# A two-layer graph network on one core: expert results scattered to the tokens' places, and layer 1's edge loop in a written order

## The chip, the cores and the metric

The kernel runs on one core of a Trainium2 chip. The metric is the device time of the whole program in microseconds (us); lower is better. The core's engines are TensorE (PE; its weight loads are listed apart as PEld), VectorE (DVE), ScalarE (ACT), GpSimd (POOL) and SyncE (SP). Each runs its instructions in order. SP issues most of the transfers here, ACT some, and POOL issues all that are addressed by a list of indices.

## What is computed

There are 6250 nodes of 256 channels and 100000 edges, sorted by their destination. The network has two layers, and each has a graph part, an attention part and a mixture of experts (MoE).

```
xn = layernorm(x)
x  = x + gnn0(xn) + linear_attention(xn)         # layer 0
x  = x + moe0(layernorm(x))                      # 32 experts, the best one per token, relu
xn = layernorm(x)
x  = x + gat(xn) + mix(xn)                       # layer 1
x  = x + moe1(layernorm(x))                      # 16 experts, the best two per token
```
```
gat:  h = x @ W;  e = leaky(h_l[own] + h_r[other])         # 4 heads of 64
      att = softmax of e over the edges of one node;  out[own] += att * h[other]
mix:  k, v = layernorm of each of 8 heads of x;  out = x @ (k^T v / N) + x
moe1: y = x + sum of the 2 chosen experts' (relu(x w1 + b1) w2 + b2) * weight
      out = layernorm(y) * gamma + beta
```

In `moe1` the x inside is the layernormed token, so the experts' output is added to that token, normed once more, and then added to the stream.

## The kernel before

**Tiles.** The nodes make NT = 49 tiles of 128 rows (the last one is short). The stream `xs` lies in SBUF for most stages. The edges make TS = 782 tiles of 128. Layer 1's edge loop works in chunks of GT = 32 edge tiles (25 chunks), and each chunk in groups of 8 tiles (98 groups).

**Stages.** Load and first norm; layer 0's edge loop; dispatch of layer 0's experts ("f0"); these experts; the rows of layer 1 (`layer1_rows`); layer 1's edge loop; dispatch of layer 1's experts ("f1"); these experts; the final gather and layernorm.

**Dispatch and experts.** `dispatch` norms the tokens, computes the router's logits (PE, L352), takes the best one or two experts of each token, counts places within each expert, and scatters each normed token with an indirect DMA (L398, 128 rows a time) to its place in a list `f_xs`, which is ordered by experts. At its end (L462 to L467) it works out, for all tokens, in which row of the result list `f_ys` the token's result will stand (`pi`). The experts then take tile after tile of `f_xs`, with the weights of the tile's expert: two matmul layers on PE (L1797, L1809 for f1), a bias add on DVE, and a plain store of 128 results to `f_ys` in the experts' order (by ACT for f0, by SP for f1). Whoever needs the results fetches them with indirect gathers, 128 tokens a time, by `pi`: `layer1_rows` does so with 49 gathers, and the final stage with 98, two per tile of tokens. All gathers go through one helper at line 300, so its line stands for several tiles: `xg` (layer 0's edges), `h` (layer 1's edges) and `yg` (results).

**The final stage.** Per block of 7 token tiles it loads the normed tokens `xc`, which the dispatch stored; for each of 14 gathered tiles `yg`, DVE does `xc += yg * wt` (L1832). Then come the layernorm (L119 to L124), times gamma (L1836), plus beta (L1837), plus `xs` (L1838), and the stores.

**Layer 1's rows.** For each token tile: the result of f0 is added to `xs`, the norm is taken, its transposed form is stored to `xnT_d`, h = xn @ W is computed, and rows of h with its logits are stored to `h_d` by SP. `xs` itself goes to `xs1_d`.

**Layer 1's edge loop** has four parts per chunk.
- `fetch`: 32 indirect gathers on POOL into four buffers `h8` of 8 tiles each (7 such buffers in all); then the nodes' own logits of each edge: DVE makes one-hot rows `ST` (L1282) and weights `hw` (L1273, L1275), PE multiplies them (L1288), ACT copies the 4x512 results (L1290), and ACT's queue stores them to `al_d`.
- `own_part`: loads these logits in another layout.
- `weigh`: the running maximum over the edges of a node, made by scans on DVE (L1315 to L1376), then exp on ACT (L1379).
- `gain`, per group of 8 tiles: DVE multiplies the gathered rows by the weights into `w8` (L1404), makes the one-hot matrix `S` (L1410), PE sums the rows by node into a PSUM tile `ps` (L1415, 2 such tiles), and DVE adds the sum to two places of the accumulator `acc` (L1419).

A second stream of work, `keys_values`, is a generator. `beside.step()` at the end of each group advances it 1.36 steps on average. Its first half takes transposed tokens, centres each head with a matmul by a constant matrix `away` (L1174), and sums k^T v (L1199). Its second half multiplies the tokens by the resulting matrix `kvm` (L1233), adds this to `xs1` (L1236) and stores the sum to `xs2_d`, from where the stream is loaded after the loop.

**Order.** The framework's scheduler arranges the instructions within each engine from the program's order and the buffers' reuse, and inserts the semaphores. The program of the loop gathers one chunk ahead:

```python
held, most = fetch(*chunks[0]), None
...
for i, (t0, n) in enumerate(chunks):
    ahead = fetch(*chunks[i + 1]) if i + 1 < len(chunks) else None
    most = weigh(t0, n, alz, *held, most)
    if ahead:
        alz = own_part(*chunks[i + 1])
    gain(t0, n, held[0])
    held = ahead
beside.rest()
```

Of the kernel before, what the change touches and what calls it, by code (L numbers as in the profile page):

```python
# [52 lines left out]
def gps_kernel(ctx, tc, x, src, dst, edge_weight, g0_W, g0_b, m0_WqT, m0_WkvT, m0_WpT, m0_bp,  # L53
# [257 lines left out]
    def expert_slots(name, ne, nk):  # L311

        ns = (N * nk + ne * (P - 1)) // P
        rest = ns - N * nk // P
        xs_d = tc.dram_tile([ne * CAP + rest * P, C], F32, name=name + "_xs")
        ys_d = tc.dram_tile([ns * P, C], F32, name=name + "_ys")
        for d, j in [(xs_d, ne * CAP + j * P) for j in range(rest)] + \
                [(ys_d, j * P) for j in range(ns - rest, ns)]:
            nc.sync.dma_start(d[j:j + P, :], zero)
        return ns, xs_d, ys_d  # L320

    def dispatch(name, fb, fw, pps, ne, nk, bt, rw, rb, ns, xs_d, top, yi, finals, stored=None):

        mask = fb.tile([P, ne, bt + 1], F32, name="d_mask")
# [11 lines left out]
        kf = fb.tile([P, NT, nk], F32, name="d_kf")  # L338
        nc.vector.memset(kf[:, NT - 1, :], -1.0)

        def logits(t0):
            n = min(bt, NT - t0)
            finals(t0, n)
            xn = fw.tile([P, bt, C], F32, name="xn", bufs=3)
            layernorm(fw, xs[:, t0:t0 + n, :], xn, n)
            if stored is not None:
                nc.scalar.dma_start(stored[:, t0:t0 + n, :], xn[:, :n, :])
            lp = pps.tile([P, bt, ne], F32, name="lp")
            for i in range(n):
                xT = transposed(fw, pps, xn[:, i, :], "xT")  # L350
                for c in range(2):
                    nc.tensor.matmul(lp[:, i, :], xT[:, c, :], rw[:, c, :], start=c == 0, stop=c == 1)  # L352
# [5 lines left out]
        def put(t0, xn, lg, turn):  # L358
            n = min(bt, NT - t0)
            ti = fw.tile([P, bt, 8], U32, name="ti")  # L360
            full_ = n if t0 + n < NT else n - 1
            for i in range(n):
                r = rows(t0 + i)
                nc.vector.max(top[:r, t0 + i, :], lg[:r, i, :])
                nc.vector.max_index(ti[:r, i, :], top[:r, t0 + i, :], lg[:r, i, :])
            if full_:
                nc.vector.tensor_copy(kf[:, t0:t0 + full_, :], ti[:, :full_, :nk])
            if full_ < n:
                nc.vector.tensor_copy(kf[:LAST, NT - 1, :], ti[:LAST, full_, :nk])
# [3 lines left out]
                kf[:, t0:t0 + n, :, None].to_broadcast([P, n, nk, ne]), op=OP.is_equal)  # L373
# [20 lines left out]
            for i in range(n):  # L394
                t = t0 + i
                r = rows(t)
                for k in range(nk):
                    st = nc.gpsimd.indirect_dma_start(  # L398
                        out=xs_d, in_=xn[:r, i, :], in_offset=None,
# [45 lines left out]
        for e in range(0, ne, 8):  # L445
            q, eng = ((nc.sync, SP), (nc.scalar, ACT))[e // 8 % 2]
            for r in group_values(tail, e, eng, ne * CAP - P):
                st = q.dma_start(xs_d[ds(r, P), :], zero)
                tc.declare_no_dep(st.ins, group=name, reason="rows behind the tokens' ones")
                tc.add_to_no_dep_group(name, st.ins)  # L450

        sh = fb.tile([ne, ne], F32, name="d_sh")
        nc.vector.tensor_sub(gend, gend, gn[:, 0:1])
        nc.vector.tensor_scalar(gend, gend, float(P), None, op0=OP.mult)
        nc.vector.tensor_scalar(sh, ident[:ne, :ne], gend, None, op0=OP.mult)
        sp = pps.tile([P, ne], F32, name="lp")
        nc.tensor.matmul(sp, ones[:ne, :], sh, start=True, stop=True)
        ss = fb.tile([P, ne], F32, name="d_ss")
        nc.vector.scalar_tensor_tensor(ss, iota[:, :ne], -float(CAP), sp, op0=OP.mult, op1=OP.add)
        for k in range(nk):  # L460
            oh = fb.tile([P, NT, ne], F32, name="d_oh")
            nc.vector.tensor_tensor(oh, iota[:, None, :ne].to_broadcast([P, NT, ne]),  # L462
                                    kf[:, :, k:k + 1].to_broadcast([P, NT, ne]), op=OP.is_equal)
            nc.vector.tensor_tensor(oh, oh, ss[:, None, :].to_broadcast([P, NT, ne]), op=OP.mult)
            row_ = fb.tile([P, NT], F32, name="d_row")
# [1421 lines left out]
```

## Time and profile before

| what | us |
|---|---|
| time, 3 runs | 4258.5, 4259.78, 4265.85; median 4259.78 |
| the profiled execution | 4279.39 |
| its span, first to last instruction | 4277.6 |

The profiled execution is 19.6 us longer than the median. Its mean granted TensorE clock is 0.747. The stages in it:

| stage | from | to | us |
|---|---|---|---|
| load and norm | 0 | 136 | 136 |
| layer 0's edge loop | 136 | 1325 | 1189 |
| f0 dispatch | 1325 | 1484 | 159 |
| f0 experts | 1484 | 1701 | 217 |
| layer 1's rows | 1701 | 1878 | 177 |
| layer 1's edge loop | 1878 | 3425 | 1547 |
| f1 dispatch | 3425 | 3621 | 196 |
| f1 experts | 3621 | 4101 | 480 |
| final gather and layernorm | 4101 | 4278 | 177 |

The profile's lines are read like this. A group (part 5 of the page) names line, engine, operation, tiles (output <- inputs) and count; after the bar stand the busy time, the mean time of one instruction in ns, the idle time of the engine just before instructions of that group, and what ended most of that idle time. The releaser "remote" means that a semaphore from elsewhere ended it, and "issue" that nothing the profile shows did. A timeline has start, length, engine and line, and in brackets the idle time before with its releaser. A line of the stretches has, for each engine, busy us and the number of instructions, then the granted clock, the share of DMA time and GB/s.

### The profile page before, as it was taken

The numbers are of one execution on the slowest core, as the hardware profiler recorded it, in microseconds if no ns is written. First come the engines' busy times: TensorE is split into PE (matmuls) and PEld (weight loads), VectorE is DVE, ScalarE is ACT, GpSimd is POOL, SyncE is SP. The second block draws the span as 40 slices with busy tenths as digits, with TensorE's granted clock in tenths as the row PEclk, the third lists the DMA queues.
The fourth block names the chain that finished last, engine by engine and source line by source line (L and its number), as shares of the span: only waits on it lengthen the run. The fifth ranks groups of instructions, "written<-read, shape, count | busy, mean of one in ns | idle before, by whom it ended". The sixth has DMA issues, their size and how long they took to land. (4 is left out here: it accounts for less than half of the span.)

```text
span 4277.6 us, 40881 instructions
## 1 busy us (share of the span) xinstructions
PE 2514.4 (59%) x10553; PEld 1822.0 (43%) x10553; DVE 2102.2 (49%) x6180; ACT 596.0 (14%) x1582; POOL 1826.0 (43%) x1864
## 2 busy tenths in 40 slices
PE   5455655677776487654554554555454444999920
PEld 4334444555555354531323333332233333888820
DVE  5345444445445666833544554554454654222247
ACT  3100000000001122221221221011010011222200
POOL 0566666566562400434445444544554245000046
PEclk9777877777786565777777777677786655999965
DMA  6643333233331344764433443454453163655644
GB/s 201 193 124 104 105 102 101 83 97 96 100 96 38 133 141 118 200 169 126 124 114 110 128 117 103 123 160 140 131 144 84 44 251 134 185 182 182 185 149 128
DMA packets 371451, 560.63 MB, mean 131 GB/s; under 512 B 106308, under 2 KB 259557, under 8 KB 370943
## 3 DMA queue, kind: packets, MB, share of 16 engines
q0 software_dynamic: 89760, 245.19, 20.5%
q1 hardware_dynamic: 243446, 273.73, 20.4%
q10 hardware_dynamic: 37992, 38.89, 2.8%
q8 instruction: 93, 1.52, 0.2%
q14 instruction: 160, 1.30, 0.1%
HBM read 440.48 MB, written 117.09 MB: 130 GB/s over the span
## 5 line engine op out<-in xcount | busy, mean ns | idle before, releaser
L300 POOL DMA_INDIRECT h<-h_d,idx x782 | 745.1, 953 | 814.2 <-DVE brk L1266 238.9
L300 POOL DMA_INDIRECT xg<-xw_d,idx x782 | 756.4, 967 | 550.0 <-issue 211.9
L1415 PE MATMUL ps<-w,S 128*128 128x260 f32 x1564 | 432.1, 438 | 374.4 <-DVE S L1410 256.7
L1415 PEld LDWEIGHTS ps<-w,S 128*128 128x128 f32 x1564 | 335.3, 219 | 488.5 <-DVE S L1410 281.8
L300 POOL DMA_INDIRECT yg<-f_ys,pi x147 | 168.3, 1145 | 813.1 <-SPq L1820 490.9
L802 PE MATMUL ps<-xg,S 128*128 128x256 f32 x1564 | 457.4, 439 | 81.2 <-DVE S L799 45.7
L802 PEld LDWEIGHTS ps<-xg,S 128*128 128x128 f32 x1564 | 333.4, 225 | 166.3 <-issue 59.1
L805 DVE SCALAR_TENSOR_TENSOR acc<-ps,in,acc 128x256 f32 x392 | 187.7, 479 | 387.6 <-remote 234.0
L1419 DVE SCALAR_TENSOR_TENSOR acc<-ps,in,acc 128x260 f32 x196 | 94.3, 481 | 556.6 <-remote 525.1
L1288 PE MATMUL p<-ST,hw 128*4 128x512 f32 x392 | 230.2, 700 | 178.9 <-DVE ST L1282 71.1
L398 POOL DMA_INDIRECT f_xs<-xn,d_pi x147 | 155.6, 1059 | 250.5 <-ACT xT L133 78.0
L799 DVE TENSOR_SCALAR S<-iota,lo,wt 128x128 f32<-128x128 f32 x782 | 242.9, 349 | 0.1
L1404 DVE TENSOR_TENSOR w<-h,exi 128x2048 f32<-128x2048 f32 x98 | 222.7, 2272 | 11.7 <-ACT exi L1379 11.7
L1809 PE MATMUL y<-w,h 128*128 x856 | 215.0, 392 | 11.2 <-ACT h L1802 10.1
L1797 PEld LDWEIGHTS hT<-xTt,w 128*128 128x128 f32 x1712 | 211.4, 194 | 6.1 <-ACT xTt L133 0.5
L1797 PE MATMUL hT<-xTt,w 128*128 128x128 f32 x1712 | 212.1, 277 | 0.2 <-ACT xTt L133 0.2
L1290 ACT COPY a<-p 4x512 f32<-4x512 f32 x196 | 111.3, 571 | 662.2 <-PE p L1288 272.3
L1805 DVE TENSOR_SCALAR h<-hT,b1T 128x128 f32<-128x128 f32 x214 | 74.8, 350 | 253.2 <-ACT h L1802 252.4
L1809 PEld LDWEIGHTS y<-w,h 128*128 128x128 f32 x856 | 149.0, 189 | 45.6 <-ACT h L1802 23.5
L1288 PEld LDWEIGHTS p<-ST,hw 128*4 128x4 f32 x392 | 24.1, 88 | 315.2 <-issue 147.7
L749 PE MATMUL ctx<-v,k 128*128 128x129 f32 (+1 forms) x196 | 44.2, 362 | 172.4 <-ACT v L747 118.2
L131 PE MATMUL tr<-ident,xt 128*128 128x128 f32 x350 | 84.7, 330 | 89.0 <-DMA xt<-f_xs 88.2
(344 smaller groups left out, 3979.3 us busy)
## 6 DMA issues: line engine op xcount, KB each, us to landing
w<-in_L_ffn_w SPq DMA_DIRECT2D x123, 512.0 KB
lob<-lob_d SPq DMA_DIRECT2D x97, 512.0 KB
xT<-xnT SPq DMA_DIRECT2D x196, 128.0 KB
xt<-f_xs SPq DMA_DIRECT2D x107, 128.0 KB
f_ys<-y SPq DMA_DIRECT2D x107, 128.0 KB
xnT<-xT SPq DMA_DIRECT2D x98, 128.0 KB
xg<-xw_d,idx POOLq DMA_INDIRECT x782
h<-h_d,idx POOLq DMA_INDIRECT x782
```

The source lines that it names most:

```text
L300: nc.gpsimd.indirect_dma_start(out=o, out_offset=None, in_=tab, in_offset=bass.IndirectOffsetOnAxis(ap=idx, axis=0))
L398: st = nc.gpsimd.indirect_dma_start(out=xs_d, in_=xn[:r, i, :], in_offset=None, out_offset=bass.IndirectOffsetOnAxis(ap=pi[:r, t, k:k + 1] ...
L799: nc.vector.tensor_scalar(S[:, i, :], iota, lo0[:, t:t + 1], wt0[:, t:t + 1], op0=OP.is_equal, op1=OP.mult)
L802: nc.tensor.matmul(ps, S[:, i, :], xg[:, i, :], start=i == 0, stop=i == n - 1)
L805: nc.vector.scalar_tensor_tensor(a, ps, m[:, b:b + 1], a, op0=OP.mult, op1=OP.add)
L1288: nc.tensor.matmul(p4[:, :w], hw, ST[:, j:j + w], start=True, stop=True)
L1290: nc.scalar.copy(a4[:, :w], p4[:, :w])
L1404: nc.vector.tensor_tensor(w8[:, :m, :C].rearrange("p i (k d) -> p i k d", k=4), hg[u // 8][:, :m, :C].rearrange("p i (k d) -> p i k d", k= ...
L1415: nc.tensor.matmul(ps, S[:, i, :], w8[:, i, :], start=i == 0, stop=i == m - 1)
L1419: nc.vector.scalar_tensor_tensor(a, ps, k[:, q:q + 1], a, op0=OP.mult, op1=OP.add)
L1797: nc.tensor.matmul(hT[:, f, :], w1[:, c, f * P:(f + 1) * P], xT[:, c, :], start=c == 0, stop=c == 1)
L1809: nc.tensor.matmul(yp, h[:, f, :], w2e[:, f * C:(f + 1) * C], start=f == 0, stop=f == nf - 1)
```

## The change

It has two parts.

**Results scattered by the experts' tiles.** Each row of `f_xs` gets extra words behind its 256 channels: the row in `f_ys` where this token's result belongs and, for f1, the token's weight for this expert and a flag that is 1 in its first copy and 0 in its second. Rows without a token carry a row number beyond the list. The dispatch so makes one normed tile per choice, copied on ACT, and works out the weights per group of tiles instead of once at its end; the search for result rows (L462 to L467) goes. A tile of experts scatters its results with an indirect DMA on POOL (`give_back`) to the tokens' places. For f1 it multiplies by the weight first and adds the token times its flag, so the normed tokens are no longer stored. `layer1_rows` and the final stage load results with plain transfers on SP (`results`), 4 and 7 tiles at once. In the final stage one add per block replaces 14 multiply-adds. The beta term is added to `xs` beside the experts.

**Layer 1's loop.** Its order is now the written one (`manual_schedule`), with gathers two chunks ahead. The product is made in place in `h8` (8 buffers), so there is no `w8`. `ps` and `S` have four buffers, and the sums of a chunk are added to `acc` during the next one (`added`). Own logits of a chunk go to one PSUM tile of 32 rows, with one copy and one store. In `keys_values` the heads are centred on DVE from rows `xr_d`, which `layer1_rows` stores by ACT's queue; its second half moves into the dispatch of f1 (`finals`), its rate is 1.1, and the stream is loaded from `xs1_d`.

The diff, cut to its core:

```diff
+    def give_back(name, ys_d, xt, y):
+        st = nc.gpsimd.indirect_dma_start(
+            out=ys_d, in_=y, in_offset=None,
+            out_offset=bass.IndirectOffsetOnAxis(ap=xt.bitcast(I32)[:, C:C + 1], axis=0),
+            bounds_check=ys_d.shape[0] - 1, oob_is_err=False)
...
+    def results(t, ys_d, k, t0, n):
...
+            nc.sync.dma_start(t[:, :whole, :], ys_d[r0:r0 + whole * P, :].rearrange(
+                "(t p) c -> p t c", p=P))
...
             finals(t0, n)
-            xn = fw.tile([P, bt, C], F32, name="xn", bufs=3)
-            layernorm(fw, xs[:, t0:t0 + n, :], xn, n)
-            if stored is not None:
-                nc.scalar.dma_start(stored[:, t0:t0 + n, :], xn[:, :n, :])
+            xn = [fw.tile([P, bt, rw_], F32, name=f"xn{k}", bufs=2 if nk == 2 else 3) for k in range(nk)]
+            layernorm(fw, xs[:, t0:t0 + n, :], xn[0][:, :, :C], n)
+            for k in range(nk):
+                if k:
+                    nc.scalar.copy(xn[k][:, :n, :C], xn[0][:, :n, :C])
+                nc.vector.tensor_copy(xn[k].bitcast(I32)[:, :n, C], ids[:, k, t0:t0 + n])
...
+            if nk == 2:
...
+                nc.scalar.activation(df[:, :n], df[:, :n], AF.Exp)
...
+                nc.vector.tensor_mul(xn[1][:, :n, C + 1], df[:, :n], xn[0][:, :n, C + 1])
...
-        for k in range(nk):
-            oh = fb.tile([P, NT, ne], F32, name="d_oh")
...
-            nc.vector.tensor_tensor(yi[:, k * NT:(k + 1) * NT], row_, pi[:, :, k], op=OP.add)
...
-                        nc.scalar.dma_start(ys_d[i * P:(i + 1) * P, :], y)
+                        give_back(name, ys_d, xt, y)
...
-                for t in range(t0, t0 + n):
-                    yg = mw.tile([P, C], F32, name="yg", bufs=8)
-                    gather(yg, ys_d, pi[:, t:t + 1])
-                    nc.vector.scalar_tensor_tensor(xs[:, t, :], yg, 0.0, xs[:, t, :],
-                                                   op0=OP.max, op1=OP.add)
+                yg = mw.tile([P, 4, C], F32, name="yg")
+                results(yg, ys_d, 0, t0, n)
+                nc.vector.scalar_tensor_tensor(xs[:, t0:t0 + n, :], yg[:, :n, :], 0.0,
+                                               xs[:, t0:t0 + n, :], op0=OP.max, op1=OP.add)
...
+                nc.scalar.dma_start(xr_d[:, t0:t0 + n, :], xn[:, :n, :])
...
-                                    nc.tensor.matmul(cen[:, t, h, :], xT[:, t, h, :], away,
-                                                     start=True, stop=True)
+                            nc.vector.tensor_reduce(sm[:, :8 * n], heads(xr), AX.X, OP.add)
+                            nc.vector.scalar_tensor_tensor(heads(xr), over(sm), -1.0 / 32, heads(xr),
+                                                           op0=OP.mult, op1=OP.add)
...
-                    h8 = gw.tile([P, 8, CR], F32, name="h8", bufs=7)
+                    h8 = gw.tile([P, 8, CR], F32, name="h8", bufs=8)
...
-                        p4 = pps.tile([4, 4 * P], F32, name="p4", bufs=2)
-                        nc.tensor.matmul(p4[:, :w], hw, ST[:, j:j + w], start=True, stop=True)
-                        a4 = gw.tile([4, 4 * P], F32, name="a4")
-                        nc.scalar.copy(a4[:, :w], p4[:, :w])
...
+                        nc.tensor.matmul(p4[:, :w], hw[:, i, :], ST[:, j * P:j * P + w],
+                                         start=i == 0, stop=i == nj - 1)
+                a4 = gw.tile([32, 4 * P], F32, name="a4")
+                nc.scalar.copy(a4, p4)
...
+            def added(t0, pss):
...
-                    w8 = gw.tile([P, 8, CR], F32, name="w8", bufs=2)
...
+                    next(due, None)
...
-                    ps = pps.tile([P, CR], F32, name="ps", bufs=2)
+                    ps = pps.tile([P, CR], F32, name="ps", bufs=4)
...
-            beside = Steps(keys_values(), 1.36)
+            beside = Steps(keys_values(), 1.1)
...
+            with tc.manual_schedule():
+                hgs, lgs, most, due = [], [], None, iter(())
+                for i in range(len(chunks) + 2):
+                    if i >= 2:
+                        t0, n = chunks[i - 2]
+                        most, fc = weigh(t0, n, hgs[i - 2], own_part(t0, n), *lgs[i - 2], most)
+                        due = gain(t0, n, hgs[i - 2], fc, due)
+                    if i < len(chunks):
+                        hgs.append(rows_to(*chunks[i]))
+                        lgs.append(own_logits(*chunks[i]))
+                for _ in due:
+                    pass
+                beside.rest()
...
-        nc.sync.dma_start(xs[:, t0:t0 + CH, :], xs2_d[:, t0:t0 + CH, :])
+        nc.sync.dma_start(xs[:, t0:t0 + CH, :], xs1_d[:, t0:t0 + CH, :])
...
+                            nc.vector.tensor_add(xs[:, t:t + m, :], xs[:, t:t + m, :], mix[:, :m, :])
...
+                            nc.vector.scalar_tensor_tensor(y, y, xt[:, C + 1:C + 2], xf,
+                                                           op0=OP.mult, op1=OP.add)
+                            give_back("f1", ys_d, xt, y)
...
-                            gather(yg, ys_d, pi[:, k * NT + t:k * NT + t + 1])
-                            nc.vector.scalar_tensor_tensor(xc[:, t - t0, :], yg, wt[:, k, t:t + 1],
-                                                           xc[:, t - t0, :], op0=OP.mult, op1=OP.add)
+                    xc, yg = (fw.tile([P, CH, C], F32, name=q, bufs=3) for q in ("xc", "yg"))
+                    for k, q in enumerate((xc, yg)):
+                        results(q, ys_d, k, t0, CH)
+                    nc.vector.tensor_add(xc, xc, yg)
```

## The prediction

> **What bounds the kernel now.** I read the stretches first (busy time of each engine per stage), because the change touches three stages that have different limits. Columns: stretch, its length, busy us (instructions) of PE, PEld, DVE, ACT, POOL, granted TensorE clock, DMA share, GB/s.
>
> ```profile
> 1980.00:3425.00 1445.00, 730.76 (x2448) 448.68 (x2447) 746.70 (x1927) 196.24 (x469) 691.24 (x726) 0.75 0.41 117
> 3425.00:3621.00 196.00, 82.22 (x364) 72.39 (x364) 109.73 (x521) 24.59 (x65) 102.91 (x98) 0.50 0.55 196
> 3621.00:4101.00 480.00, 430.92 (x2782) 380.67 (x2782) 119.72 (x321) 105.17 (x321) 0.00 (x0) 0.98 0.57 176
> 4101.00:4278.00 177.00, 0.00 (x0) 0.00 (x0) 119.80 (x273) 3.38 (x8) 117.27 (x98) 0.51 0.48 148
> ```
>
> These are layer 1's edge loop (it begins at 1878, where the gathers of its first chunk go out; 1547 us in all), the dispatch of its experts, the experts, and the final gather with the layernorm. In the loop no engine is busy much over half the time, so something waits in turn. The experts are PE's (431 of 480). The end is DVE and POOL in alternation.
>
> Then the groups, to see what the loop's POOL and DVE wait for; the last column is idle time before the group and its releaser.
>
> ```profile
> L300 POOL DMA_INDIRECT h<-h_d,idx x782 | 745.1, 953 | 814.2 <-DVE brk L1266 238.9
> L1404 DVE TENSOR_TENSOR w<-h,exi 128x2048 f32<-128x2048 f32 x98 | 222.7, 2272 | 11.7 <-ACT exi L1379 11.7
> L1419 DVE SCALAR_TENSOR_TENSOR acc<-ps,in,acc 128x260 f32 x196 | 94.3, 481 | 556.6 <-remote 525.1
> ```
>
> POOL's 782 gathers stand idle for 814 us. DVE stands idle for 557 us before its adds of the group sums. Last the timelines of POOL, PE and DVE around one chunk's end:
>
> ```profile
> 2531.38 0.94 POOL L300 DMA_INDIRECT h<-h_d,idx  x1 [0.30 <-issue]
> 2555.35 1.17 POOL L300 DMA_INDIRECT h<-h_d,idx  x1 [23.03 <-DVE w L1404]
> ```
> ```profile
> 2520.45 3.56 PE L1415 MATMUL ps<-w,S 128*128 128x260 f32 x15 [2.39 <-issue]
> 2524.34 0.38 PE L1415 MATMUL ps<-w,S 128*128 128x260 f32 x1 [0.34 <-issue]
> ```
> ```profile
> 2537.70 0.49 DVE L1419 SCALAR_TENSOR_TENSOR acc<-ps,in,acc 128x260 f32 x1 [17.12 <-remote]
> ```
>
> A gather run of POOL ends at 2532.3, then POOL idles 23 us until DVE's product L1404 frees a buffer of rows. DVE had stood at L1419 for 17 us although PE's records of these sums end at 2524.7. It went on 5.4 us after the gather run ended. The same distance stands at three other chunk ends (runs ending at 2153.2, 2219.2, 2283.3; adds at 2158.6, 2224.5, 2288.7). So a sum reaches DVE late while POOL issues gathers back to back, and DVE, stopped there, does not free POOL's buffers. Each chunk is 40 us of gathers and some 22 us of POOL waiting, 62 us in all; why the sums are late the trace does not show.
>
> **The loop after.** Removed: `added` takes a chunk's sums during the next chunk (four ps buffers), so the stop at L1419 goes. The product is made in the gathered rows, so a row buffer is freed by PE's last matmul of its group rather than by DVE, and eight buffers hold two chunks. What is late next:
> - POOL: gathers back to back take 0.95 + 0.30 = 1.25 us (the timeline), 32 of them 40 us. 782 x 1.25 = 978 us is the floor.
> - DVE per chunk, from the rows by form: four groups of product 2.28, S 1.22, two adds 0.96, ST 0.75, hw 0.43: 5.6 x 4 = 22.6, less some 2 where instructions overlap; weigh about 10.5 (2538.1 to 2548.5 in the timeline, with others' work between); keys_values at 1.1 steps a group, 4.4 a chunk, one tile pair: sum 0.68, centring 0.68 (priced by the 128x512 add), sum of squares 0.68, two u at 0.415, small ones 0.4: 3.3. Together 33 to 36, below 40.
> - PE: the rows L1415 (432.1 busy) and L1288 (230.2) make 662 in the loop, 27 a chunk, and both stay; PE is not the bound. ACT's copies of logits fall from 8 of 0.57 to 1, SP gains nothing but xr rows in place of xT.
>
> The new wait: POOL's gather of chunk i waits for PE's matmuls of chunk i-2. Queued behind it are only later gathers. DVE can start weigh 5 us after a run has ended (landing), the product of group 0 some 14 later, so PE has freed the first buffer near 26 to 30 of the next run's 40 us. If that release comes at once, POOL never stops: 978 plus ends. If it comes as late as DVE's sums did, POOL stops at the run's end and goes on 5 us later. The rows nearest are exactly those 5.4, 5.4, 5.3 and 5.5 us, so I take one pause of 5 per chunk: 45 x 24.4 chunks = 1100. To this come the start and the tail: last rows landing 5, the rest of gain, weigh and gain again 23 + 24, adds 2: about 55. **Loop 1155, so -392.** From below: no pause, some 1035 to 1060. From above: DVE's fixed order idles at every ACT exp and at each late release twice a chunk, 50 to 52 us a chunk, 1270 to 1330.
>
> **The end.** Ninety-eight gathers go (98 x 1.25 = 122 us of POOL), seven loads of two 0.9 MB tiles come in on SP. DVE loses L1832 (98 x 0.477, 45.1) and the bet adds (14.1, now beside the experts), gains seven adds at 2.0 (14.1): 119.8 - 45.1 = 75. Traffic is 12.8 MB in and 6.4 out, at 200 to 250 GB/s (the best slices of the page) 77 to 96. Start and last store 10 to 20. I take **100, so -77** (-85 to -60).
>
> **Dispatch of layer 1's experts** (196). Added: the mixing matmuls, 196 at 0.33 = 65 us of PE, which is 82 of 196 busy, so mostly beside; 25 adds at 0.68 = 17 of DVE; thirteen copies of the second row on ACT; per group of four an Exp beside the layernorm's Sqrt, two table loads of 1.28 (that row) = 33 of ACT, where DVE waits for both; some 10 of small DVE work. Removed: the closing L462-L467 (six of 0.97 and two small: 6) and 6.4 MB of xn stores. Scatters stay 98. POOL has 98 x 1.35 = 132 there. I take **+30**; below +10 if ACT and PE hide, +60 if nothing does.
>
> **The rest.** Experts f1: a multiply-add on DVE (0.48) and a copy on ACT (0.37) per tile of 4.5 us, a scatter of about 1 us on a POOL that does nothing there (0.00), in place of SP's store: 0, from -5 to +15 (the xt rows grow by 3 words, and the result leaves one step later). Experts f0: the store leaves ACT's queue for POOL's: 0 +- 5. Layer 1's rows (177): 49 gathers, 13 stores on ACT's queue and 13 loads of 512 KB on SP's; DVE's work there stays: -5, from -15 to +15. The zero stores at the start, 48 fewer: 0 to -10, taken as 0. Sum: -392 - 77 + 30 - 5 = -444. The profiled execution took 4279.4, so 3835; it is 19.6 above the median of the runs, 4259.8, so on that footing **3815**.
>
> **Rivals.**
> 1. *DVE's fixed order is the bound* (50 to 52 a chunk, loop 1300). For it: 36 us of work against 40 leaves 4 for all its waits on ACT, and nothing may be reordered. Against: DVE's waits besides L1419 are short (11.7 before L1404 in total). Time 3815 + 150 = 3965.
> 2. *The sums still stop the loop* (it does not do what it says). If the late release grows with the time since the last pause, PE's buffers come free no sooner than DVE's did: the loop stays near 1500, time 4165. For: the worst lag in the waits is 25.7 us. Against: POOL then has a pause, and a pause is what released the sums.
> 3. *Slower: POOL and the compute in lockstep.* Rows' landings may be seen as late as the sums. Then weigh of chunk i-2 begins only when the run of i-1 is over, both sets of buffers are full, and POOL waits for landing 5 and most of DVE's 33: 40 + 5 + 33 = 78 a chunk, 1903 in the loop, +356 - 52 = about 4565. It decides as soon as no group has been freed when a run ends, and costs over 62 a chunk once 22 us of compute are left then. For: z L1315 also waits for h rows, 56 us in 14 waits. Against: the longest of these is 6.7.
> 4. *DVE against POOL at SBUF.* In the end, beside the two-input ops L1836 to L1838, gathers took 2.0 instead of 0.95:
> ```profile
> 4140.74 2.03 POOL L300 DMA_INDIRECT yg<-f_ys,pi  x1 [0.30 <-issue]
> ```
> In a loop bounded by POOL each two-input DVE op that is new there would stretch a gather by its length: 25 x (0.68 + 0.83) = 38, time 3853. Against: inside the loop the mean gather is 0.953 even with L1404 and two-input adds around it. The Trainium skill, "SBUF — State Buffer", section "Who interferes with whom", says that a VectorE instruction with two SBUF inputs contends with a GpSimd instruction that reads SBUF. This trace agrees at 4140 and hardly inside the loop.
>
> **Chances.** Forecast 0.56 (its own range 3690 to 3900: loop 1060 to 1210 with the other terms' bounds), DVE's order 0.17, SBUF 0.07, late sums 0.10 (a fifth of it, 0.02, within 0.2% because the dispatch costs its bound too and the loop gains nothing), lockstep 0.08, below 3690 0.02. Range 3690 to 4080: it takes in rivals 1 and 4 and leaves out about 0.2. Faster by over 0.2% (about 8.5 us, what a measurement of this kernel can tell from no change): 0.90; within 0.02; slower 0.08.
>
> **What would show it.** Right: POOL's idle before the row gathers falls from 814 to about 250 and its releaser is PE's matmul; DVE's "remote" before the delayed adds is gone; the loop is 1155 long; the mean gather stays 0.95; the end has no indirect gathers and lasts 100; the dispatch is longer by 30. Wrong: DVE over 90% busy in the loop (rival 1), POOL pauses of 20 us per chunk (2) or of 35 with DVE's z waiting for rows (3), gathers of 1.2 us and more (4). The prediction falls first with the assumption that a late release costs a pause of 5 us and not more.

## The result, and the profile after

The changed kernel took 4159.65 us (median of 4 runs, 4132.14 to 4211.6), the kernel before 4260.17 beside it. The ratio is 0.974, with an interval of 0.9685 to 0.9795. A ratio with an interval leaves out, here and below, runs that are over 1.5% longer than the same kernel's fastest. The forecast was 3815 with a range of 3690 to 4080, so a gain came, of 100 where 445 was forecast. The profiled execution is the longest of the four: 4211.6, with a span of 4209.8. Its stages against those of the profiled execution before (us):

| stage | before | after | difference | forecast |
|---|---|---|---|---|
| load, norm, layer 0's loop, f0 dispatch | 1484 | 1500 | +16 | 0 |
| f0 experts | 217 | 232 | +15 | 0 |
| layer 1's rows | 177 | 208 | +31 | -5 |
| layer 1's loop | 1547 | 1350 | -197 | -392 |
| f1 dispatch | 196 | 270 | +74 | +30 |
| f1 experts | 480 | 548 | +68 | 0 |
| end | 177 | 102 | -75 | -77 |
| sum | 4278 | 4210 | -68 | -444 |

The stretches after, in the columns used before (stretch, length, busy us of PE, PEld, DVE, ACT, POOL, clock, DMA share, GB/s):

```profile
1940.00:3290.00 1350.00, 642.83 (x2156) 411.23 (x2156) 855.08 (x2074) 139.10 (x342) 781.95 (x783) 0.74 0.43 123
3290.00:3560.00 270.00, 121.19 (x558) 107.49 (x558) 124.06 (x633) 63.59 (x110) 102.47 (x98) 0.55 0.44 144
3560.00:4108.00 548.00, 437.85 (x2782) 382.84 (x2782) 183.99 (x435) 156.59 (x428) 104.66 (x107) 0.97 0.51 153
4108.00:4210.00 102.00, 0.00 (x0) 0.00 (x0) 78.32 (x177) 3.39 (x8) 0.82 (x1) 0.51 0.56 189
```

The experts' PE does the same 430 to 438 us of work as before, and stands still for the rest of a stage that is 68 longer. In the loop DVE is busy for 63%, POOL for 58%: again something waits in turn. The groups that answer to the three shown of before, first POOL's from the page, then DVE's from the groups of this stretch:

```profile
L300 POOL DMA_INDIRECT h<-h_d,idx x782 | 781.7, 1000 | 713.9 <-issue 399.0
```
```profile
L1435 DVE TENSOR_TENSOR h<-h,exi 128x2048 f32<-128x2048 f32 x98 | 222.9, 2274 | 3.4 <-ACT exi L1394 2.1 <-issue 1.3
L1422 DVE SCALAR_TENSOR_TENSOR acc<-ps,in,acc 128x260 f32 x196 | 95.2, 486 | 5.0 <-DVE acc L1422 0.9 <-PE ps L1445 0.7
```

DVE's idle time before the adds fell from 557 to 5, as forecast. POOL's fell only from 814 to 714, where 250 was said; but 210 of the 714 is one wait ahead of the loop's first gather, since POOL has no work left in layer 1's rows (64 before). Inside the loop its pauses of over 1 us fell from 521 to 274. The waits inside the loop (engine, line, what it waited for, us in total, times, longest):

```profile
ACT a L1306 <- remote: 507.3, 15, 39.3
DVE fc L1401 <- ACT fc L1399: 204.5, 17, 23.5
```

In place of DVE at the adds, ACT now waits in front of L1306, its copy of the own logits, and DVE waits for ACT. One chunk shows how. First PE, then ACT, DVE and POOL:

```profile
2576.48 7.05 PE L1303 MATMUL p<-ST,hw 128*32 128x512 f32 x16 [0.47 <-issue]
2616.64 9.59 PE L1445 MATMUL ps<-h,S 128*128 128x260 f32 x29 [33.10 <-DVE S L1440]
```
```profile
2608.51 0.57 ACT L1306 COPY a<-p 32x512 f32<-32x512 f32 x1 [36.38 <-remote]
2609.45 1.28 ACT L1394 ACT_TABLE_LOAD   x1 [0.37 <-ACT a L1306]
2610.75 1.00 ACT L1394 ACTIVATE exi<-z 128x32 f32<-128x32 f32 x4
```
```profile
2592.65 0.31 DVE L1391 STREAM_TRANSPOSE z<-zl 128x128 f32<-128x128 f32 x1
2611.91 0.23 DVE L1401 TENSOR_SCALAR fc<-fc,in 128x4 f32<-128x4 f32 x1 [18.95 <-ACT fc L1399]
```
```profile
2604.03 0.95 POOL L300 DMA_INDIRECT h<-h_d,idx  x1 [0.30 <-issue]
2624.12 0.95 POOL L300 DMA_INDIRECT h<-h_d,idx  x1 [19.14 <-issue]
```

PE's records of the logits end at 2583.5. POOL's run (gathers without a pause between them) ends at 2605.0. ACT's copy starts at 2608.5, 25 us behind PE and 3.5 behind POOL. The exps of the next chunk stand behind that copy in ACT's queue, though their inputs were ready at 2593.0 (L1391). DVE needs the exps, so its products come 19 us late, PE frees POOL's buffer late, 0.7 us before the next gather, and POOL pauses 19 us. This chunk takes 61 us. In the last third of the same loop the runs fell otherwise. ACT's copy mostly starts as soon as PE is done, here at 2812.8, 17 us into a run of POOL, and the pause is the one forecast:

```profile
2812.88 0.58 ACT L1306 COPY a<-p 32x512 f32<-32x512 f32 x1 [12.68 <-PE p L1303]
```
```profile
3065.30 0.95 POOL L300 DMA_INDIRECT h<-h_d,idx  x1 [0.30 <-issue]
...
3072.05 0.94 POOL L300 DMA_INDIRECT h<-h_d,idx  x1 [4.55 <-issue]
```

Most chunks up to 2744 take 59 to 61, those after 2840 mostly 45 to 48. How many take which differs from one execution to the next, and with it the time.

### The profile page after: what moved, and what is told of

It reads as the page before. It is cut to its first block, busy times and chain, and to the rows that moved or that the text cites. A ratio compares the mean times of both kernels' runs of the same rounds, so it can differ in the third digit from the quotient of the medians.

```text
span 4209.8 us, 40726 instructions
## 1 busy us (share of the span) xinstructions
PE 2422.2 (58%) x10353; PEld 1803.2 (43%) x10353; DVE 2218.2 (53%) x6303; ACT 617.3 (15%) x1577; POOL 1877.2 (45%) x1894
## 5 line engine op out<-in xcount | busy, mean ns | idle before, releaser
L300 POOL DMA_INDIRECT h<-h_d,idx x782 | 781.7, 1000 | 713.9 <-issue 399.0
L1445 PE MATMUL ps<-h,S 128*128 128x260 f32 x1564 | 445.1, 445 | 674.6 <-DVE S L1440 455.7
L1445 PEld LDWEIGHTS ps<-h,S 128*128 128x128 f32 x1564 | 344.1, 225 | 782.4 <-DVE S L1440 474.4
L326 POOL DMA_INDIRECT f_ys<-y,xt x175 | 180.1, 1029 | 633.0 <-DVE y L1855 418.3
L1435 DVE TENSOR_TENSOR h<-h,exi 128x2048 f32<-128x2048 f32 x98 | 222.9, 2274 | 3.4 <-ACT exi L1394 2.1
L1303 PE MATMUL p<-ST,hw 128*32 128x512 f32 x392 | 178.4, 604 | 34.7 <-DVE ST L1298 17.8
L139 PE MATMUL pr<-wp,aT 128*128 128x256 f32 x196 | 73.5, 512 | 125.1 <-ACT aT L133 63.9
L131 PEld LDWEIGHTS tr<-ident,xt 128*128 128x128 f32 x350 | 44.4, 160 | 222.6 <-issue 206.8
```

The source lines that it names most:

```text
L131: nc.tensor.transpose(p[:, c, :], t[:, c * P:(c + 1) * P], ident)
L300: nc.gpsimd.indirect_dma_start(out=o, out_offset=None, in_=tab, in_offset=bass.IndirectOffsetOnAxis(ap=idx, axis=0))
L326: st = nc.gpsimd.indirect_dma_start(out=ys_d, in_=y, in_offset=None, out_offset=bass.IndirectOffsetOnAxis(ap=xt.bitcast(I32)[:, C:C + 1], ...
L1303: nc.tensor.matmul(p4[:, :w], hw[:, i, :], ST[:, j * P:j * P + w], start=i == 0, stop=i == nj - 1)
L1435: nc.vector.tensor_tensor(v, v, ex[:, u:u + m, :, None].to_broadcast([P, m, 4, 64]), op=OP.mult)
L1445: nc.tensor.matmul(ps, S[:, i, :], h8[:, i, :], start=i == 0, stop=i == m - 1)
```

## The experiments

The theory: PE's results are seen late while POOL issues gathers back to back (shown for part of each run, see the last section); the change removed DVE's stop behind them and put ACT's copy, with the exps behind it, in the same place. The rival: DVE's fixed order sets the chunk. For the other stages: buffers that scatters hold too long, against wider rows or more work.

The runs went to two kinds of chip. On one the kernel before takes 4260 to 4270, as in the first runs; on the other 3851 to 3854. All ten traces of the first kind have waits put down to "remote" (138 to 202 in each), and none of the eight of the other has one. A time is compared only with the kernel before on its own chip, and "4260" and "3850" name the kinds below.

**results_only** (on 3850): the results part, with the loop of before.

> Only the results part of the change; layer 1's loop, the mix add and the stream's store are those of before. Theory A (the profile of after read by stages): final stage about 102 instead of 177 (-75), experts f1 548 instead of 480 (+68), f0 experts and layer 1's rows +15 and +31, dispatch f1 +10 to +30, so some 4310 +- 30, slower than before. Theory B (the losses in the experts' stages come with the loop part, which leaves other data and other buffers behind): final stage -75 alone, some 4185.

3962.68 against 3854.48, ratio 1.0268 (1.0234 to 1.0303). The part is a loss of 108 by itself: the end takes 102, the f1 experts 551. Theory A.

**loop_only** (on 3850): the loop part, with results gathered as before.

> Only the loop part of the change (with the mix add in the dispatch, and the rows stored for it); results are gathered as before. Theory A: the loop falls from 1547 to about 1350 (1250 to 1450, by how many chunks take 60 us and how many 46), the dispatch of f1 rises by 40 to 60 because its token loads stand behind the experts' weights on SP, final stage 177, experts 480: 4120 +- 60. Theory B (the results part shortens the loop, for instance by fewer gathers on POOL): the loop stays at about 1500, 4250.

3644.67 against the same 3854.48, 0.9451 (0.9419 to 0.9483). This matches neither text: the loop takes 1074 here, not 1350, because this kind of chip has no late sums at all. Its loop, and that of the kernel before as results_only has it:

```profile
1686.00:2760.00 1074.00, 619.74 (x2156) 402.15 (x2156) 857.19 (x2070) 138.98 (x342) 783.47 (x782) 0.79 0.53 155
```
```profile
1740.00:3081.00 1341.00, 755.33 (x2540) 448.81 (x2540) 784.04 (x2032) 219.70 (x505) 752.18 (x783) 0.76 0.47 138
```

POOL issues all 782 gathers from 1686 to 2708 without a pause of 1 us. The loop is then POOL's, as the floor of the prediction has it.

**copy_later** (on 3850) and **copy_later_2** (again on 3850):

```diff
-                a4 = gw.tile([32, 4 * P], F32, name="a4")
-                nc.scalar.copy(a4, p4)
-                nc.scalar.dma_start(al_d[t0 // GT].rearrange("k (j s) -> (k j) s", s=4 * P), a4)
...
                         due = gain(t0, n, hgs[i - 2], fc, due)
+                    if last is not None:
+                        stored_logits(*last)
...
-                        lgs.append(own_logits(*chunks[i]))
+                        lg, last = own_logits(*chunks[i + 1])
+                        lgs.append(lg)
```

`stored_logits` holds the three lines taken out. The edit also moves the tile `brk` into `weigh` and gives two small tiles a fourth buffer.

> The changed kernel with one edit: the own logits are made one chunk earlier, and ACT copies and stores them after the group work of the next chunk, so that ACT's copy no longer stands ahead of the exps of the next chunk. Theory A (the copy waits for PE's signal, which comes only some 4 us after the gather run has ended, and DVE waits behind it for the exps, 19 us a chunk): that wait goes, chunks take 42 to 47 instead of 60, loop 1080 to 1200, time 3950 to 4020. Theory B (DVE's fixed order bounds the chunk; ACT's copy is late only because DVE is): chunks stay at 55 to 60, time within 30 of 4150.

> The kernel with ACT's copy of the own logits later, once more, for a chip with late signals. Theory A: where the changed kernel's loop takes 1350 to 1480 (chunks of 60), this one takes some 1200 to 1250 (chunks of 46), time 4020 to 4060; where it takes 1070, this one takes 1070 as well. Theory B (all of the gain of the four edits came from the three others): loop above 1300 on a chip with late signals.

3722.54 against 3854.48 (0.9657, interval 0.9619 to 0.9695) and 3707.56 against 3851.1 (0.9638). The loops are 1068 and 1070, equal to the 1072 that the unedited loop of xt8 takes on such a chip. So the edit does nothing where there are no late signals, and 0.965 is about what the change itself is worth there. The later copy alone did not run on 4260.

**xt8** (on 3850):

```diff
-                            xt = fv.tile([P, xs_d.shape[1]], F32, name="xt", bufs=4)
+                            xt = fv.tile([P, xs_d.shape[1]], F32, name="xt", bufs=8)
```

> The changed kernel with eight instead of four buffers for the token tiles in the experts of f1. Theory A (a token tile is held until its results have been scattered, and SP's load of the next one waits for that, 226 us in 93 waits): the experts fall from 548 to 480 to 495, time 55 to 65 below the changed kernel. Theory B (the wider rows and the scatter's own traffic slow the loads): the experts stay at 530 to 550.

3673.9 against 3854.48, 0.9527 (0.9495 to 0.9558). The f1 experts take 476, against 543 in copy_later on the same chip, both from the first transpose to the last result; the whole run is 49 shorter. In the changed kernel SP's load of a tile and PE wait like this:

```profile
SPq L1831 <- DMA f_ys<-y,xt: 226.5, 93, 4.5
```
```profile
PE tr L131 <- DMA xt<-f_xs: 120.9, 46, 24.4
```

With eight buffers the first wait falls to 0 and PE's to 37.8 (SP and PE of xt8):

```profile
SPq L1831 <- ACT xTt L133: 10.6, 35, 0.7
```
```profile
PE tr L131 <- DMA xt<-f_xs: 37.8, 42, 2.7
```

The scatter reads its row numbers from the token tile, so the tile lives on until the scatter's DMA is done. In the kernel before it was free after the transpose. Theory A; the wider rows cost nothing that shows.

**before_again, after_again, w2_spread, all_four** (on 4260). The third puts the loads of the experts' weights behind the token loads of each group; the fourth has that, xt8, copy_later and, in layer 1's rows, the load of results one block ahead:

```diff
-                for e in range(ne):
-                    nc.sync.dma_start(
-                        w2[:, e * wn:(e + 1) * wn].rearrange("p (c f) -> p c f", f=C),
...
                             nc.vector.tensor_add(xs[:, t:t + m, :], xs[:, t:t + m, :], mix[:, :m, :])
+                        for e in range(t0 // 2, min(t0 // 2 + 2, ne)):
+                            nc.sync.dma_start(
+                                w2[:, e * wn:(e + 1) * wn].rearrange("p (c f) -> p c f", f=C),
```
```diff
-                yg = mw.tile([P, 4, C], F32, name="yg")
-                results(yg, ys_d, 0, t0, n)
+                for t in (t0, t0 + 4):
+                    if t < NT and t not in ygs:
+                        ygs[t] = mw.tile([P, 4, C], F32, name="yg", bufs=2)
+                        results(ygs[t], ys_d, 0, t, min(4, NT - t))
+                yg = ygs[t0]
```

> The kernel before, once more with a profile, on the chip of the next runs. Theory A (in the first execution's trace, signals of PE reached the other engines late while POOL issued gathers; on the chip of the last runs no such waits stood in the loops): where DVE's adds of the sums show no long wait of that kind, layer 0's loop takes about 1005 and layer 1's about 1340, total some 3850; where they do, 1181 and 1544, total some 4260. Theory B (the difference of 400 us between the two chips is TensorE's clock alone): PE-bound stages differ most, the experts of f1 by some 10 per cent, and the loops by less.

> The changed kernel, once more. Theory A: without the late signals the loop has no pauses of POOL, 1070; experts of f1 540, dispatch 265, end 102, total some 3740, 0.97 of the kernel before; with them chunks of 60 and 46 us, total 4130 to 4210. Theory B (PE's clock): the loop stays above 1300 on any chip.

> The changed kernel, with the sixteen loads of 512 KB of the experts' weights spread over the first eight groups of the dispatch of f1, behind each group's token loads on SP. Theory A (DVE waits 19 us and POOL 42 us after the first group because the token loads stand behind 8 MB of weights): the dispatch falls from about 265 by 20 to 35. Theory B (the dispatch is bound by its own work per group, and the weights' time is only moved): within 8 of the changed kernel.

> The changed kernel with four edits: eight buffers of token tiles in the experts of f1, ACT's copy of the own logits later, the weights' loads spread, and in layer 1's rows the loads of results issued one block ahead. Theory A: -68 from the experts, -20 to -35 from the dispatch, 0 to -20 from the rows, and from the copy 0 where the loop has no pauses and -100 to -200 where it has: some 3620 on a chip without late signals, some 3900 with them. Theory B (the gains are taken back by the next stage): less than 60 below the changed kernel.

The kernel before took 4275.7 with its profile, layer 0's loop 1171 and layer 1's 1542, and DVE's "remote" waits are there:

```profile
DVE acc L1419 <- remote: 494.5, 30, 27.4
```

Against before_xn2 (below, on 3850) the gathers of layer 0's loop take 1170 instead of 1001 and layer 1's loop 1543 instead of 1345, 367 of the 416 between the two kinds. The f1 experts, from the first transpose to the last result, take 469 to 475 on both kinds in kernels with that stage unchanged. So most of the difference is in the two loops, not in PE-bound work. The changed kernel took 4178 to 4327, ratio 0.9846 (0.977 to 0.9923), with a loop of 1477 in its profile; the median of all four runs, 4250.3, is 0.9956 of the kernel before. w2_spread took 4148 to 4304 (median 4239.69), which does not set it apart from the changed kernel. Its dispatch is 261 against 268 in after_again, Theory B: the stall after the first group is only moved. all_four: 3961.4 against 4269.27, 0.9265 (0.9233 to 0.9298), faster than both kernels. Of its edits only the later copy touches the loop (w2_spread, without it, has 1457), which falls to 1210:

```profile
1918.00:3128.00 1210.00, 693.06 (x2156) 441.67 (x2156) 857.22 (x2072) 136.73 (x342) 775.00 (x783) 0.75 0.48 138
```
```profile
2579.06 1.21 POOL L300 DMA_INDIRECT h<-h_d,idx  x1 [5.45 <-issue]
...
2625.69 1.16 POOL L300 DMA_INDIRECT h<-h_d,idx  x1 [5.38 <-issue]
```

From 2532 on POOL runs 41 us and pauses 5 to 6 in nearly every chunk: 47 a chunk. In these pauses PE's last matmul on the buffer had ended 18 to 24 us before the gather: POOL too sees PE late. The f1 experts take 483 (546 in after_again), the rows 192 (212).

**pool_pause** (on 3850) and **pool_pause_2** (on 4260): work added to POOL in the middle of each run.

```diff
                 for u in range(0, n, 8):
+                    if u == 16:
+                        for _ in range(30):
+                            nc.gpsimd.memset(rest_, 0.0)
```

> The changed kernel with 30 small memsets on POOL after the first 16 of every 32 row gathers: work added on the busiest engine, some 4 to 8 us a chunk, without any dependence on the rest. Theory A (PE's signals reach ACT late only while POOL issues gathers back to back, and a break lets them through): where POOL pauses 19 us at the end of its runs, the copy of the own logits is released in the break, that pause falls to 5 or less, chunks take 50 to 55 instead of 60, and the loop is shorter by 50 to 200 in spite of the added work; where there are no late signals, the loop is longer by the memsets, 25 x 4 to 8 = 100 to 200. Theory B (the copy is late for a reason that has nothing to do with POOL): the loop is longer by 100 to 200 on any chip.

> The changed kernel with 30 small memsets (about 7 us) on POOL after the first 16 of every 32 row gathers, once more. Where the kernel before takes some 4270 (late signals): Theory A (POOL's back-to-back gathers hold PE's signals up) gives a loop of 1150 to 1300, below the changed kernel's 1350 to 1480 in spite of the added work, and ACT's copy released within the break; Theory B (they have nothing to do with POOL) a loop of 1450 to 1650. Where the kernel before takes some 3850, both give 1219 as in the run before.

The break is 6.8 us, 24 of them some 160. On 3850 the loop is 1219, 147 longer than in xt8, as both theories say there, and the time 3858.98 against 3851.1. On 4260, where the unedited loop of after_third takes 1437, it is 1297:

```profile
1914.00:3211.00 1297.00, 698.72 (x2156) 416.11 (x2156) 854.93 (x2072) 138.84 (x342) 890.69 (x1503) 0.74 0.44 129
```

Time 4128.89 against 4266.98 (0.9668, 0.9629 to 0.9707), where the changed kernel has 0.984. Adding some 160 us of work to the busiest queue took 140 off the loop. Theory A, with one correction: the copy now starts within 1 us of PE's last record in 21 of 25 chunks, yet only 8 of 25 in the break. PE's own matmuls are stretched instead. These came out one at a time while gathers ran:

```profile
2328.20 0.59 PE L1450 MATMUL ps<-h,S 128*128 128x260 f32 x1 [2.00 <-DMA h<-h_d,idx]
2331.02 0.59 PE L1450 MATMUL ps<-h,S 128*128 128x260 f32 x1 [2.24 <-issue]
2333.82 1.01 PE L1308 MATMUL p<-ST,hw 128*32 128x512 f32 x1 [2.21 <-issue]
```

**no_gathers** (on 3850) and **no_gathers_2** (on 4260): later chunks use the rows of the first two again.

```diff
-                        gather(h8[:, i, :], h_d, idx1[:, t:t + 1])
+                        if t < 2 * GT:
+                            gather(h8[:, i, :], h_d, idx1[:, t:t + 1])
```

> The changed kernel, but only the first two chunks' rows are gathered; later chunks use the same eight buffers again, so the edges' rows are wrong and POOL is idle. Theory A (the late signals come from POOL's gathers): no wait of the kind remote ahead of ACT's copy on any chip, and the loop shows what DVE, ACT and PE need, 36 to 42 a chunk, some 950 to 1030. Theory B (they come from the chip or from DVE's order, not from POOL): waits of 30 us ahead of ACT's copy stay where they stood, the loop stays above 1300 there.

> The changed kernel with only the first two chunks' rows gathered, so the edges' rows are wrong and POOL is idle, once more. Where the kernel before takes some 4270: Theory A gives a loop of some 970 to 1000 without waits of the kind remote ahead of ACT's copy; Theory B a loop above 1300 with them. Where it takes some 3850, both give 967.

The loops are 967 and 984 (one run each, 3598.18 and 3802.68): the two kinds of chip differ by 2% once POOL is still, against 1072 and 1350 to 1477 with gathers. On 4260 every copy but the first two, made while POOL still gathered, now starts when PE's last matmul ends; its releaser is PE, not "remote":

```profile
ACT a L1309 <- PE p L1306: 257.5, 22, 20.2
```

Theory A. Issuing and the gathers' transfers went together, so these runs do not say which of the two it is. The stretch on 4260 shows what is left, DVE at 92%:

```profile
2050.00:2800.00 750.00, 504.57 (x1788) 328.02 (x1787) 689.29 (x1695) 119.97 (x292) 0.00 (x0) 0.85 0.21 68
```

Copies follow each other by 36 to 37 us there: DVE's chunk, so the rival of the fixed order at 50 to 52 falls.

**after_third, all_four_2** (on 4260, with pool_pause_2):

> The changed kernel once more, with the kernel before on the same chip. Theory A: where the kernel before takes some 3850, loop 1070, dispatch 262, experts 538, some 3735, 0.97 of before; where it takes some 4270, loop 1350 to 1480 and 4130 to 4330. Theory B (the loop's length follows TensorE's clock): loop above 1250 everywhere.

> The changed kernel with the four edits, once more. Theory A: where the kernel before takes some 3850, 70 to 100 below the changed kernel there, some 3645; where it takes some 4270, 3960 again. Theory B (without late signals the edits are taken back by the next stage): within 40 of the changed kernel.

4256.23 (0.984, 0.9793 to 0.9887) and 3968.7 (0.9269, 0.9229 to 0.9308), as before; 4256.23 is the median of all eight runs and 0.9975 of the kernel before. So by the medians the changed kernel gains 0.3 to 2.4% on 4260 (its profiled loops are 1350, 1477 and 1437). The profiled execution of all_four_2 is its longest, 4044.72, and its loop 1293: some pauses of 10 to 17 are back in it, so late results still cost something there. The rival of the clock falls with xt8's loop of 1072 and, on 4260, the 984 of no_gathers_2. In after_third's trace 15 of 25 copies start 25 to 27 us after PE's last recorded matmul, and all of these 3.9 to 4.4 after a run's end.

**before_xn2** (on 3850): the kernel before with two buffers for the normed tokens in the dispatch of f1 instead of three.

> The kernel before with two instead of three buffers for the normed tokens in the dispatch of f1. Theory A (the changed dispatch is long because its two tiles per group have only two buffers each, so DVE waits for scatters): the dispatch rises from 205 by 20 to 50, with POOL's scatters in runs of 16 and pauses of about 11 between them. Theory B (the mixing matmuls, the exps and the weights' loads make it long): it stays within 8 of 205.

Its dispatch takes 230 (the kernel before: 205 on 4260; its profile on 3850 was not taken), and POOL's scatters come in runs of 16 with pauses of 10 to 13, where the kernel before has 4 to 6 for most:

```profile
3093.84 1.00 POOL L398 DMA_INDIRECT f_xs<-xn,d_pi  x1 [13.31 <-DVE d_pi L393]
...
3124.96 0.96 POOL L398 DMA_INDIRECT f_xs<-xn,d_pi  x1 [10.08 <-DVE ln_rs L122]
```

Theory A in kind. The size is open: 25 compares two kinds of chip, and on 4260 this stage of the kernel before also holds 76 us of "remote" waits (before_again), which before_xn2 does not have. The one run took 3908.64 against 3851.1 on its own chip (13 runs, 3836 to 3861), 57 more, with only this stage edited. So two buffers cost 25 to 57, beside the 65 to 70 that the changed dispatch is longer on 4260. results_only has 235 in this stage (two buffers and the exps), loop_only 225 (three buffers and the mixing).

## Why the prediction was wrong

**The step that failed** is "the new wait: POOL's gather of chunk i waits for PE's matmuls ... it goes on 5 us later". The prediction had seen that PE's results come late while POOL gathers, named it as unexplained, and then followed it only to POOL's buffers. It reaches PE's other consumers too. The changed kernel has another one, ACT's copy of the logits, and the written order puts the next chunk's exps behind it. So the pause was 17 to 20, not 5, in 11 of 24 chunks of the profiled execution (18 in after_again, 15 in after_third), and the loop 1350 where 1155 was said. By the prediction's own terms: gathers with their short gaps 1012 (978 said), pauses 274 (122), the tail after the last gather 62 (55 with the start). The 250 of idle time said for POOL does not fit these terms: 782 x 0.30 and 122 make 357. With that copy out of the way, the loop is 1210 in the first run of all_four and the pause 5.4: the mechanism and its size were right for the wait that was considered, though 1210 is all_four's loop with three other edits outside it. The queue behind the moved wait was ACT's, and it was not read.

**Rival 2** came true in kind (late results of PE still stop the loop, the logits in place of the sums; 4165 was said, 4159.65 measured). Its condition, a release that grows later with the time since POOL's last pause, is what the copies show (last section). The number is partly an accident: its loop of 1500 was too long, and the other stages cost what it did not have.

**DVE per chunk, 33 to 36**: 36 to 37 by no_gathers. Right. **The floor, 978**: 1021 from the first gather to the last in loop_only, because the gathers of the changed loop take 1.00 us instead of 0.953. That is rival 4's size (38) by luck, with another operation; see the last section.

**The end, -77**: -75, right. The seven loads were enough and DVE is busy for 78 of 102.

**f1 experts, 0 (-5 to +15)**: +68, outside its bounds. The prediction asked what the scatter costs on POOL, which was free, and not how much longer the scatter keeps its source: the token tile, with four buffers. xt8 shows it: 476 against 543.

**f1 dispatch, +30 (+10 to +60)**: +74. The mixing was counted; two things were not. The token loads that moved here stand behind 16 loads of weights on SP, and DVE waits 19 for the second group's; spreading the loads gave only 7 back. And the normed tokens are now two tiles per group with two buffers each instead of one with three; that is 25 to 57. The rest is not taken apart.

**Layer 1's rows, -5 (-15 to +15)**: +31. Plain loads stand in SP's queue behind stores that wait for ACT and DVE (38 us at L1131, 29 at L1095); POOL's gathers had a queue of their own. Loading one block ahead takes 14 to 20 back. The loop part has a share too: on 3850 the rows take 184 in before_xn2, 195 in loop_only, which only adds the stores of `xr_d`, and 198 in results_only. **f0 experts, 0**: +15 in the profile; results_only against before_xn2 on 3850 has 222 to 203 (190 in loop_only, where the stage is unchanged too). No edit was made for it alone.

**The sum**: on chips without late signals the loop gains some 270 (1341 to 1072, two thirds of the 392 said), and the results part, forecast as a gain of some 60, costs 108 in all. The two parts measured alone, -210 and +108, add up to -102; together they give -132 and -144 (0.965, copy_later). The 30 to 40 between are not explained.

## What to carry to other kernels

A result seen late holds up everything behind whoever waits for it, so after a wait is removed, list all other consumers of the same producer and read what stands behind each in its queue. A transfer that reads a tile keeps the tile: where a store is moved, made slower or given its addresses from another tile, count the buffers that it now holds. A part that pays in one stage (75 at the end) should be measured alone: here it lost 108 in all while its partner won 210.

## What the runs showed of the hardware

On some chips here PE's results reach ACT, DVE and POOL up to 27 us late, or PE issues one matmul per 2 to 3 us, while POOL issues indirect gathers back to back; on others the changed kernel shows none of it (in xt8 all 25 copies start within 1 us). It goes when the gathers go, and shrinks with a break in them. A run of gathers does no harm at first. In after, after_again, after_third, w2_spread and pool_pause_2, past the loop's first two chunks, the logits' last matmul ended at most 17.2 us after the start of POOL's run in 25 cases: ACT's copy began at most 8.1 us later, in 19 of them within 1 us. In 79 cases it ended 17.5 us or more into the run, and 77 of these copies began 11 us or more later. What holds PE up on these chips, why only there, and what turns at 17 us stays open. It makes the time of the kernel before differ by 10% between chips (4267 and 3851).

Gathers are longer beside DVE's one-hot rows (one SBUF tile, in place). In the changed loop:

```profile
2575.80 1.82 POOL L300 DMA_INDIRECT h<-h_d,idx  x1 [0.31 <-issue]
2577.93 1.85 POOL L300 DMA_INDIRECT h<-h_d,idx  x1 [0.30 <-issue]
```
```profile
2575.68 0.75 DVE L1298 TENSOR_SCALAR ST<-ST,pcol 128x1024 f32<-128x1024 f32 x1
2576.75 0.75 DVE L1298 TENSOR_SCALAR ST<-ST,pcol 128x1024 f32<-128x1024 f32 x1
```

The gathers of this loop exceed 0.95 us by 39 in all; the 77 that run beside L1298 hold 34 of it, and 24 of these fall on the 29 that meet two such operations. The written order puts four in a row. The kernel before ran them spread out and mostly while POOL paused (5 us of excess). The Trainium skill, "SBUF — State Buffer", section "Who interferes with whom", says that a tensor_scalar can enter a mode in which VectorE takes the port pair that it shares with GpSimd, and that the other engine then fully blocks. The trace agrees with that sentence as far as the gathers' lengths go; which mode the operation was in is not shown. The products L1435 beside the gathers, whose second input lies in PSUM, cost 1.2 us in all.
